# Sharing out the side work of a selective-scan kernel: by what is left of a unit instead of by a running credit

## The chip, the cores and the metric

The kernel runs on one core of one Trainium2 chip. The metric is device time in microseconds for one execution. The kernel before took 2837.61 us, the median of 3 runs that lie between 2833.27 and 2842.39 us.

## What is computed

The input has 2 sequences of 1024 tokens with 512 channels. A selective state-space layer with a state of 128 per channel comes first, then a residual and a layer normalisation, then a gated feed-forward layer of hidden width 2048, again with residual and normalisation. All of it is float32.

```
xn    = x * rsqrt(mean(x*x) + 1e-6) * norm_w
xn    = xn * sigmoid((xn @ select_proj_w.T + b) * select_gate)
xp    = xn @ x_proj_w.T                  # delta, B, C
delta = softplus(xp_delta @ dt_proj_w.T + dt_proj_b)
h     = exp(delta * A) * h + (delta * xn) * B      # for every token, 512 x 128 states
y     = sum over the state of h * C
x     = layernorm(x + (y + x * D_param) @ out_proj_w.T)
x     = layernorm(x + (silu(x @ w_gate.T) * (x @ w_up.T)) @ w_down.T)
```

## The kernel before, in words

**The scan and its places.** The 2048 tokens are cut into 64 steps of 32 tokens. A step has 16 pieces of work, so the main loop (L666 on, `for k in range(NG)`) runs 1024 times. One turn is called a place here, and its number modulo 8 is `r`; eight places are half a step. In each place TensorE (PE) makes the products `bu` (L689) and, for the next place, the decay exponents `a` (L407); ScalarE (ACT) takes their exponentials into `a_sb` (L414); VectorE (DVE) adds the carried state to the first column (L708) and runs one scan over 1024 elements (L709). GpSimd (POOL) spreads the operands (`ddt`, `du`, L378 and L388), one operation for each place. The two buffers of `bu` let PE work on the next place while DVE scans this one, and no further.

**The y products.** After a half's scans its outputs are summed by PE in `y_round` (L426): 12 matmuls at r = 1, 12 at r = 4 and 8 at r = 7 (`ROUNDS`). These three values of `r` get no side work.

**Side work.** Everything else on PE is written as generators: `pre` prepares the next lot of tokens (units ss, sel, xp, b, z, uT, t), `post` makes the layer's output for a tile of 128 tokens (units zT, op), `ffn` makes the feed-forward layer of that tile (units x1T, gu, d). A unit is one group of matmuls into the single PSUM tile `m` (pool `ps_m`, one buffer). It is cut into parts by `yield`: a `gu` unit has 8 parts of two matmuls, a `d` unit 16 parts of one, `op` 8, `sel`, `xp` and `ss` 4, `z` 2, the transposes 2, `t` 1. At the letter P a unit waits to be begun, at H it can go on, at E it waits for work of other engines, and what follows an E (the copy out of PSUM, the normalisation) is issued by `others` or `give_back` in a later place. A tile's post and ffn have 10 and 98 parts; a lot's `pre` has 39.

**How much in each place.** `work.tensor()` runs one part. It goes on with the unit that holds PE, or begins the first one that stands at P, and does nothing if the holder waits at an E; so at most one unit is in hand in a place. `PARTS` gives r = 0 four parts and r = 2, 3, 5 and 6 three each, 16 in eight places. What is not used stays as credit, up to 6, and at most 4 parts run in a place.

**Tiles and lots.** 64 places make one tile of 128 tokens. A lot has 256 tokens, two tiles, except the first two lots, which have one tile each. `pre` of the next lot is begun at a lot's first place, at the front of the list.

**The end.** After the last place the remaining y products are made, the rest of the list runs without places (L746, `while work.gens`), and the last tile's post and ffn end the program.

Of the kernel before, what the change touches and what calls it, by code (L numbers as in the profile page):

```python
# [18 lines left out]


ROUNDS = ((), (0, 1, 2), (), (), (3, 4, 5), (), (), (6, 7))
PARTS = (4, 0, 3, 3, 0, 3, 3, 0)
RMS_EPS = 1e-6
LN_EPS = 1e-5

# [9 lines left out]
def kernel(  # L35
# [25 lines left out]
    NF = wgu_s.shape[0]  # L61
    NM = D // P
# [79 lines left out]
    def col(group, m):  # L142
        return vec[:, group, m : m + 1]
# [10 lines left out]

    made = {}

    def misc(name):
        return bank_pool[0].tile([P, 512], FP, tag="m", name=name)


# [3 lines left out]
    def pre(c):  # L164

        t0, n = lots[c]
        n_j, n_s = n // P, n // S
# [15 lines left out]
        def matmuls(ps, w, m, rhs):  # L183
            for k in range(NM):
                nc.tensor.matmul(  # L185
                    ps[:, 0:n], w[:, k, ts(m, P)], rhs[:, k, :],
                    start=(k == 0), stop=(k == NM - 1),
                )
                yield "H" if k + 1 < NM else "E"
# [7 lines left out]
        for m in range(NM):  # L197
            nc.scalar.activation(xT[:, m, :], xT[:, m, :], AF.Copy, scale=col(V_NORM, m))
        yield "P"
        ps = misc(f"ss_{c}")  # L200
        for k in range(NM):
            nc.tensor.matmul(  # L202
                ps[:, 0:n], ones, u[:, k, :], start=(k == 0), stop=(k == NM - 1)
# [12 lines left out]


        for m in range(NM):
            ps = misc(f"sel_{c}_{m}")
            yield from matmuls(ps, sel_w, m, xn)  # L220
            nc.scalar.activation(
                u[:, m, :], ps[:, 0:n], AF.Relu,
                bias=neg[:, 1, m : m + 1], scale=neg[:, 0, m : m + 1],
            )
            nc.scalar.activation(
                dt[:, m, :], ps[:, 0:n], AF.Abs, bias=gate_b[:, m : m + 1], scale=col(V_GATE, m)
            )
            yield "P" if m + 1 < NM else "E"
# [9 lines left out]
            decay()  # L238

        for g, dst in ((0, low), (2, c_sb)):  # L240
            ps = misc(f"xp_{c}_{g}")
            yield from matmuls(ps, xp_w, g, xn)
            nc.scalar.copy(dst, ps[:, 0:n])
            yield "P"

        ps = misc(f"b_{c}")
        for j in range(n_j):
            for k in range(NM):
                nc.tensor.matmul(  # L249
# [12 lines left out]
        yield "P"  # L262

        for a in range(0, NM, 2):
            ps = misc(f"z_{c}_{a}")
            for m in (a, a + 1):
                nc.tensor.matmul(  # L267
                    ps[:, ts(m - a, n)], dt_w[:, ts(m, P)], low, start=True, stop=True
                )
                yield "H" if m == a else "E"  # L270
            for m in (a, a + 1):
                z = ps[:, ts(m - a, n)]
                nc.scalar.activation(u[:, m, :], z, AF.Relu, bias=col(V_DTB, m))
                nc.scalar.activation(dt[:, m, :], z, AF.Abs, bias=col(V_DTB, m))  # L274
            yield "P" if a == 0 else "E"
# [4 lines left out]

        for j in range(n_j):
            yield "P"
            ps = misc(f"uT_{c}_{j}")
            for m in range(NM):
                nc.tensor.transpose(ps[:, ts(m, P)], u[:, m, ts(j, P)], ident)
                if m == 1:
                    yield "H"
            yield "E"
            t = pre_pool.tile([P, D], FP, tag="row", name=f"uT_{c}_{j}")
            nc.scalar.copy(  # L290
                t.rearrange("p (g m c) -> p m g c", g=4, m=NM),
                ps.rearrange("p (m g c) -> p m g c", m=NM, g=4),
            )
            for st in range(4):
                nc.sync.dma_start(
                    ub_d[t0 // S + 4 * j + st, :, :, 0, :].rearrange("g t q -> t g q"),
                    t[ts(st, S), :].rearrange("t (g q) -> t g q", g=4),
                )
            if c == 0:
                load(0)  # L300
                diag(0, 0)
                diag(0, 1)
        yield "P"
        ps = misc(f"t0_{c}")
        for m in range(NM):
            nc.tensor.matmul(
                ps[0:n_s, ts(m, P)],
# [89 lines left out]
    def place(k):  # L397
        h, r = divmod(k, 8)
        m, pair = divmod(r, 2)
        return h, m, pair  # L400
# [47 lines left out]
    def post(tt):  # L448

        zT = post_pool.tile([P, NM, P], FP, tag="zT", name=f"zT_{tt}")  # L450
        nc.sync.dma_start(zT, x_q.rearrange("(m p) t -> p m t", p=P)[:, :, ts(tt, P)])
        yield "E"
        yield "E"
        nc.gpsimd.tensor_tensor(zT, zT, dq.unsqueeze(2).to_broadcast([P, NM, P]), ALU.mult)
        yield "E"
        yield "P"
        ps = misc(f"zT_{tt}")
        for s in range(4):
            nc.tensor.transpose(ps[:, ts(s, P)], yrs[tt][:, s, :], ident)
            if s == 1:  # L460
                yield "H"
        yield "E"
        z = zT.rearrange("p m (s t) -> p s m t", t=S)
        nc.vector.tensor_tensor(
            z, z, ps.rearrange("p (s m t) -> p s m t", m=NM, t=S), ALU.add
        )
        x1 = post_pool.tile([P, D], FP, tag="x1", name=f"x1_{tt}", bufs=4)
        nc.sync.dma_start(x1, xf[tt])
        yield "P"
        ps = misc(f"op_{tt}")  # L470
        for half in (slice(0, 256), slice(256, 512)):
            for k in range(NM):
                nc.tensor.matmul(  # L473
                    ps[:, half], zT[:, k, :], out_w[:, k, half], start=(k == 0), stop=(k == NM - 1)
                )
                yield "H" if half.start == 0 or k + 1 < NM else "E"
        nc.vector.tensor_tensor(x1, x1, ps, ALU.add)
        yield "E"
        yield from normalize(x1, f"a{tt}")
        work.add(ffn(tt, x1))  # L480

    def normalize(t, name):
# [10 lines left out]
    def ffn(tt, row):  # L493
# [17 lines left out]
        fetch(4)  # L511
        x1T = ffn_pool.tile([P, NM, P], FP, tag="x1T", name=f"x1T_{tt}")
        yield "P"
        ps = misc(f"x1T_{tt}")
        for m in range(NM):
            nc.tensor.transpose(ps[:, ts(m, P)], row[:, ts(m, P)], ident)
            if m == 1:
# [6 lines left out]
        for f in range(0, NF, 2):  # L524
            fetch(at + 4)
            yield "P"
            ps = misc(f"gu_{tt}_{f}")
            for b in range(2):
                w = pieces[at + b].rearrange("p (a k h) -> p a k h", a=2, k=NM)
                for a in range(2):  # L530
                    for k in range(NM):
                        nc.tensor.matmul(  # L532
                            ps[:, ts(2 * a + b, P)], w[:, a, k, :], x1T[:, k, :],
                            start=(k == 0), stop=(k == NM - 1),
                        )
                        if k % 2:
                            yield "E" if a and b and k + 1 == NM else "H"
            at += 2
            gu = ffn_pool.tile([P, 2, 2 * P], FP, tag="gu", name=f"gu_{tt}_{f}", bufs=2)
            nc.scalar.copy(gu, ps.rearrange("p (a t) -> p a t", a=2))  # L540
            work.add(silu(gu, hid[:, f : f + 2, :], f"{tt}_{f}", ready), front=True)
        while len(ready) < NF // 2:
            yield "E"
        for half in range(2):
            fetch(at + 4)
            yield "P"
            ps = misc(f"d_{tt}_{half}")
            for f in range(NF):
                if f == NH:
                    fetch(at + 6)  # L550
                w = pieces[at + f // 4].rearrange("p (f d) -> p f d", f=4)
                nc.tensor.matmul(  # L552
                    ps[:, 0:HD], hid[:, f, :], w[:, f % 4, :],
                    start=(f == 0), stop=(f == NF - 1),
                )
                yield "H" if f + 1 < NF else "E"
            part_of = row[:, ts(half, HD)]
            nc.vector.tensor_tensor(part_of, part_of, ps[:, 0:HD], ALU.add)
            at += 4
# [38 lines left out]
    class Work:  # L598


        def __init__(self):
            self.gens, self.holder = [], None

        def add(self, gen, front=False):
            item = [gen, next(gen)]
# [23 lines left out]
        def tensor(self):  # L629

            if self.holder is not None:
                if self.holder[1] != "H":
                    return False
                self.step(self.holder)
                return True
            for item in self.gens:
                if item[1] == "P":
                    self.holder = item
                    self.step(item)
                    return True  # L640
            return False

# [5 lines left out]
    work = Work()  # L648
# [13 lines left out]
    for b in range(2):  # L662
        decay_exp(0, b, decay_mm(0, b))

    pres, begun, credit = {}, set(), 0
    for k in range(NG):  # L666
        h, m, pair = place(k)
        st, i = divmod(h, 2)
        r = k % 8

        if PARTS[r]:
            work.give_back()
        if r == 0:
            hs[h] = half_pool.tile([P, 256, S], FP, tag="h", name=f"h_{h}")
            if i == 0:
                c = lot_of[st]
# [10 lines left out]
        for b in range(2):  # L687
            g = 2 * pair + b
# [26 lines left out]
        if h:  # L715
            for b in ROUNDS[r]:
                y_round(h - 1, b)
        credit = min(credit + PARTS[r], 6)
        for _ in range(min(credit, 4) if PARTS[r] else 0):
            if not work.tensor():  # L720
                break
            credit -= 1

        j, r4 = divmod(k, 4)
        if r4 == 3:
# [93 lines left out]
```

## Time and profile before

| what | us |
|---|---|
| profiled execution, device time | 2842.96 |
| its span, first to last instruction | 2841.2 |
| start of the first scan, start of the last scan | 43.2, 2758.35 |
| PE matmul busy | 2727.4 |
| DVE busy | 2522.9 |
| POOL busy | 1783.3 |
| ACT busy | 1549.8 |
| wait of DVE's add (L708) for PE's a (L407), in total | 80.2 |
| wait of PE's bu (L689) for DVE's scan (L709), in total | 28.3 |

The granted TensorE clock is 0.987 of full speed over the span. Busy time says how long an engine had an instruction in it; matmuls are pipelined, so PE's busy time is not work at its peak. The chain is followed back from the last instruction; its shares are of the span. In a timeline each row is one group of equal instructions that follow each other: start, duration, engine, line, operation, output and inputs, count; a float32 matmul shows as two records, so x16 is eight matmuls.

### The profile page before, as it was taken

The page shows a single profiled execution, that of the slowest core. Times are in us where ns is not written, and L with a number is a line of the kernel's source. Part 1 is how long each engine was busy: PE and PEld are TensorE (multiplying, and loading weights), DVE is VectorE, ACT ScalarE, POOL GpSimd, SP SyncE. Part 2 cuts the span into 40 slices and gives each one's busy share as a digit, 9 for nine tenths or more (in the row PEclk, how much of TensorE's full clock was granted, in tenths as well). Part 3 has the DMA queues.
Part 4 walks back from the last instruction along what each step waited for, and adds up shares of the span by engine and source line. Part 5 has one row for each costly group of instructions (what it writes and reads, how often), then busy time and mean ns, then how long its engine had stood idle before and what let it go on. Part 6 is the DMA issues. An engine that isn't in the chain of part 4 may idle for free.

```text
span 2841.2 us, 57463 instructions
## 1 busy us (share of the span) xinstructions
PE 2727.4 (96%) x22728; PEld 1484.1 (52%) x22728; DVE 2522.9 (89%) x2144; ACT 1549.8 (55%) x3105; POOL 1783.3 (63%) x2016
## 2 busy tenths in 40 slices
PE   7879999999999999999999999999999999999998
PEld 4324554555555554555544555555555555555558
DVE  2999898999999999999999999999999999999980
ACT  4546555555565455654656556555555554555442
POOL 4556675666667675775667667667576666657552
PEclk7999999999999999999999999999999999999999
DMA  2012222224223232233312333132331323332336
GB/s 75 16 30 66 86 77 79 87 73 134 86 62 116 86 121 64 83 96 105 123 43 84 105 104 104 57 100 93 112 101 47 113 87 109 101 105 96 107 103 208
DMA packets 112380, 258.67 MB, mean 91 GB/s; under 512 B 11568, under 2 KB 49456, under 8 KB 112112
## 3 DMA queue, kind: packets, MB, share of 16 engines
q1 hardware_dynamic: 112112, 254.99, 27.6%
q8 instruction: 181, 2.97, 0.4%
q14 instruction: 87, 0.71, 0.1%
HBM read 242.23 MB, written 12.71 MB: 90 GB/s over the span
## 4 chain that ended last, share of the span: by engine, by line
PE 75%; DVE 18%; issue 3%; ACT 2%; POOL 1%; DMA 0%; SPq 0%; DVEq 0%; POOLq 0%; ACTq 0%
PE bu L689 28%; PE gu L532 17%; DVE h L709 15%; PE y L426 13%; PE d L552 7%; PE a L407 4%; PE sel L185 2%; PE op L473 1%; PE xp L185 1%; DVE bu L708 1%; ACT a_sb L414 1%; PE b L249 1%; PE ss L202 0%; PE z L267 0%; DMA ub_d<-uT 0%
## 5 line engine op out<-in xcount | busy, mean ns | idle before, releaser
L709 DVE TENSOR_TENSOR_SCAN h<-a_sb,bu 128x1024 f32<-128x1024 f32 x1024 | 2341.2, 2287 | 159.2 <-POOL ddt L378 43.2
L414 ACT ACTIVATE a_sb<-a 128x496 f32<-128x496 f32 x2048 | 1089.0, 585 | 1142.6 <-PE a L407 1013.3
L689 PE MATMUL bu<-du,ub 32*128 32x512 f32 x4096 | 1198.0, 646 | 52.5 <-DVE h L709 28.3
L407 PE MATMUL a<-ddt,a_t 32*128 32x512 f32 x4096 | 1240.7, 646 | 2.8 <-ACT t L313 2.8
L378 POOL TENSOR_TENSOR ddt<-dt,hot 128x512 f32<-128x512 f32 x512 | 534.5, 1050 | 225.2 <-PE a L407 225.1
L532 PEld LDWEIGHTS gu<-x1T,w 128*128 128x128 f32 x4096 | 481.7, 192 | 232.8 <-issue 155.0
L388 POOL TENSOR_TENSOR du<-ub,hot 128x512 f32<-128x512 f32 x512 | 536.4, 1052 | 25.7 <-PE a L407 22.3
L532 PE MATMUL gu<-x1T,w 128*128 128x128 f32 x4096 | 537.3, 283 | 11.2 <-ACT t L313 4.5
L689 PEld LDWEIGHTS bu<-du,ub 32*128 32x128 f32 x4096 | 337.2, 184 | 375.8 <-issue 205.6
L426 PE MATMUL y<-h,cz 128*32 128x256 f32 x8192 | 524.7, 385 | 1.9 <-DVE h L709 1.3
L426 PEld LDWEIGHTS y<-h,cz 128*32 128x32 f32 x8192 | 227.7, 109 | 406.7 <-issue 271.9
L407 PEld LDWEIGHTS a<-ddt,a_t 32*128 32x128 f32 x4096 | 371.5, 184 | 19.9 <-ACT a_sb L414 9.6
L708 DVE TENSOR_TENSOR bu<-bu,cd 128x32 f32<-128x32 f32 x992 | 184.9, 186 | 83.1 <-PE a L407 80.2
L552 PE MATMUL d<-w,hid 128*128 128x256 f32 x1024 | 256.9, 393 | 1.1 <-ACT dt L274 1.1
L552 PEld LDWEIGHTS d<-w,hid 128*128 128x128 f32 x1024 | 183.5, 189 | 121.6 <-issue 92.5
L570 POOL TENSOR_SCALAR gu<-gu 128x256 f32<-128x256 f32 x128 | 108.3, 846 | 209.4 <-ACT gu L540 208.4
L578 POOL TENSOR_TENSOR hid<-gu,e 128x256 f32<-128x256 f32 x128 | 93.1, 728 | 141.7 <-ACT e L576 140.8
L440 POOL TENSOR_TENSOR yc<-yc,pick 128x512 f32<-128x512 f32 x64 | 66.7, 1042 | 168.7 <-ACT yc L439 168.7
L365 POOL TENSOR_TENSOR cd<-cd,h 128x256 f32<-128x256 f32 x124 | 106.5, 859 | 44.5 <-DVE h L709 44.5
L571 POOL TENSOR_TENSOR gu<-gu 128x256 f32<-128x256 f32 x128 | 93.4, 730 | 10.7
L540 ACT COPY gu<-gu 128x512 f32<-128x512 f32 x128 | 75.3, 588 | 33.5 <-PE gu L532 33.3
L323 POOL TENSOR_TENSOR dt<-dt,u 128x512 f32<-128x512 f32 (+1 forms) x36 | 41.3, 1151 | 68.7 <-ACT dt L320 68.7
(86 smaller groups left out, 1252.6 us busy)
## 6 DMA issues: line engine op xcount, KB each, us to landing
w<-in_wgu_s_dram SPq DMA_DIRECT2D x256, 512.0 KB, 3.8
w<-in_wd_s_dram SPq DMA_DIRECT2D x128, 512.0 KB, 4.0
cd<-dt_d SPq DMA_DIRECT2D x62, 256.0 KB, 4.0
ub<-ub_d SPq DMA_DIRECT2D x64, 128.0 KB, 2.0
ub_d<-bt SPq DMA_DIRECT2D x64, 64.0 KB, 1.8
ub_d<-uT SPq DMA_DIRECT2D x64, 64.0 KB, 1.8
zT<-in_x_q_dram SPq DMA_DIRECT2D x16, 256.0 KB, 4.0
x<-in_x_dram SPq DMA_DIRECT2D x16, 256.0 KB, 3.6
```

Of the source, the lines that this page charges most:

```text
L365: nc.gpsimd.tensor_tensor(cd, cd, last, ALU.mult)
L378: nc.gpsimd.tensor_tensor(ddts[j][:, m, :, :], made[lot_of[st]][0][:, a + m, toks(st)].unsqueeze(1).to_broadcast([P, 16, S]), hot[:, ts(i, ...
L388: nc.gpsimd.tensor_tensor(dus[j][:, m, :, :], uv[:, a + m, :].unsqueeze(2).to_broadcast([P, 16, S]), hot.unsqueeze(1).to_broadcast([P, 16, ...
L407: nc.tensor.matmul(ps, a_t[ts(g, 32), m, :], ddts[k // 4][ts(g, 32), m % 2, :, :], start=True, stop=True,)
L414: nc.scalar.activation(a_sb[:, k % 3, ts(b, 16), 1:], ps[:, :, 1:], AF.Exp, scale=-1.0)
L426: nc.tensor.matmul(ys[st][ts(m, 32), ts(i, 256)], cz[st % 3][:, at : at + 32], hs[h][:, ts(m, 64), ts(b, 4)], start=(i == 0 and b == 0), s ...
L532: nc.tensor.matmul(ps[:, ts(2 * a + b, P)], w[:, a, k, :], x1T[:, k, :], start=(k == 0), stop=(k == NM - 1),)
L552: nc.tensor.matmul(ps[:, 0:HD], hid[:, f, :], w[:, f % 4, :], start=(f == 0), stop=(f == NF - 1),)
L570: nc.gpsimd.tensor_scalar_max(g, g, -80.0)
L689: nc.tensor.matmul(bu[:, ts(b, 16), :], prepared[st][ts(g, 32), 1, :], dus[k // 4][ts(g, 32), m % 2, :, :], start=True, stop=True,)
L708: nc.vector.tensor_tensor(first, first, left[:, at : at + 2, i, :], ALU.add)
L709: nc.vector.tensor_tensor_scan(hs[h][:, ts(r, 32), :].rearrange("p q t -> p (q t)"), a_sb[:, k % 3, :, :].rearrange("p q t -> p (q t)"), b ...
```

## The change

Each unit now says how many parts it has when it takes its PSUM tile. A unit with four parts or less left, the one in hand among them, runs to its end in one go. A longer one runs four parts at r = 2 and 3, three at r = 5, 6 and 0, but four at r = 0 and 6 if it is begun there. The credit is gone. The matmuls, copies and transfers themselves are the same; their order on the engines is another.

```diff
-PARTS = (4, 0, 3, 3, 0, 3, 3, 0)
+PARTS = (3, 0, 4, 4, 0, 3, 3, 0)
...
-    def misc(name):
+    def misc(name, parts):
+        work.left = parts
         return bank_pool[0].tile([P, 512], FP, tag="m", name=name)
...
-            ps = misc(f"gu_{tt}_{f}")
+            ps = misc(f"gu_{tt}_{f}", 2 * NM)
...
-            ps = misc(f"d_{tt}_{half}")
+            ps = misc(f"d_{tt}_{half}", NF)
...
-            self.gens, self.holder = [], None
+            self.gens, self.holder, self.left, self.fresh = [], None, 0, False
...
             if self.holder is not None:
                 if self.holder[1] != "H":
                     return False
+                self.left -= 1
+                self.fresh = False
                 self.step(self.holder)
                 return True
             for item in self.gens:
                 if item[1] == "P":
                     self.holder = item
                     self.step(item)
+                    self.left -= 1
+                    self.fresh = True
                     return True
...
-        credit = min(credit + PARTS[r], 6)
-        for _ in range(min(credit, 4) if PARTS[r] else 0):
-            if not work.tensor():
-                break
-            credit -= 1
+        if PARTS[r] and work.tensor():
+            more = work.left
+            if more > 3:
+                more = (4 if work.fresh and r in (0, 6) else PARTS[r]) - 1
+            for _ in range(more):
+                work.tensor()
```

The other calls of `misc` get their counts in the same way (NM for ss, sel and xp, 2 for z and the transposes, 1 for t, 2 * NM for op).

More of the change, by code (lines that the diff above doesn't have):

```diff
@@ L199, in pre @@
         yield "P"
-        ps = misc(f"ss_{c}")
+        ps = misc(f"ss_{c}", NM)
         for k in range(NM):
@@ L218, in pre @@
         for m in range(NM):
-            ps = misc(f"sel_{c}_{m}")
+            ps = misc(f"sel_{c}_{m}", NM)
             yield from matmuls(ps, sel_w, m, xn)
@@ L240, in pre @@
         for g, dst in ((0, low), (2, c_sb)):
-            ps = misc(f"xp_{c}_{g}")
+            ps = misc(f"xp_{c}_{g}", NM)
             yield from matmuls(ps, xp_w, g, xn)
@@ L244, in pre @@
             yield "P"
-        ps = misc(f"b_{c}")
+        ps = misc(f"b_{c}", n_j)
         for j in range(n_j):
@@ L264, in pre @@
         for a in range(0, NM, 2):
-            ps = misc(f"z_{c}_{a}")
+            ps = misc(f"z_{c}_{a}", 2)
             for m in (a, a + 1):
@@ L282, in pre @@
             yield "P"
-            ps = misc(f"uT_{c}_{j}")
+            ps = misc(f"uT_{c}_{j}", 2)
             for m in range(NM):
@@ L303, in pre @@
         yield "P"
-        ps = misc(f"t0_{c}")
+        ps = misc(f"t0_{c}", 1)
         for m in range(NM):
@@ L456, in post @@
         yield "P"
-        ps = misc(f"zT_{tt}")
+        ps = misc(f"zT_{tt}", 2)
         for s in range(4):
@@ L469, in post @@
         yield "P"
-        ps = misc(f"op_{tt}")
+        ps = misc(f"op_{tt}", 2 * NM)
         for half in (slice(0, 256), slice(256, 512)):
@@ L513, in ffn @@
         yield "P"
-        ps = misc(f"x1T_{tt}")
+        ps = misc(f"x1T_{tt}", 2)
         for m in range(NM):
@@ L663 @@
         decay_exp(0, b, decay_mm(0, b))
-    pres, begun, credit = {}, set(), 0
+    pres, begun = {}, set()
     for k in range(NG):
```

## The prediction

> **What bounds the kernel now.** I read the page first: busy time and the chain.
>
> ```profile
> PE 2727.4 (96%) x22728; PEld 1484.1 (52%) x22728; DVE 2522.9 (89%) x2144; ACT 1549.8 (55%) x3105; POOL 1783.3 (63%) x2016
> ...
> PE 75%; DVE 18%; issue 3%; ACT 2%; POOL 1%; DMA 0%; SPq 0%; DVEq 0%; POOLq 0%; ACTq 0%
> ...
> L709 DVE TENSOR_TENSOR_SCAN h<-a_sb,bu 128x1024 f32<-128x1024 f32 x1024 | 2341.2, 2287 | 159.2 <-POOL ddt L378 43.2
> ...
> L708 DVE TENSOR_TENSOR bu<-bu,cd 128x32 f32<-128x32 f32 x992 | 184.9, 186 | 83.1 <-PE a L407 80.2
> ```
>
> The chain lies on PE and DVE in turn, so I look at single places: DVE's timeline around place 443, then PE's.
>
> ```profile
> 1226.66 2.29 DVE L709 TENSOR_TENSOR_SCAN h<-a_sb,bu 128x1024 f32<-128x1024 f32 x1
> ...
> 1229.71 2.29 DVE L709 TENSOR_TENSOR_SCAN h<-a_sb,bu 128x1024 f32<-128x1024 f32 x1
> ...
> 1232.21 2.29 DVE L709 TENSOR_TENSOR_SCAN h<-a_sb,bu 128x1024 f32<-128x1024 f32 x1
> ...
> 1234.82 2.29 DVE L709 TENSOR_TENSOR_SCAN h<-a_sb,bu 128x1024 f32<-128x1024 f32 x1
> ...
> 1237.30 2.29 DVE L709 TENSOR_TENSOR_SCAN h<-a_sb,bu 128x1024 f32<-128x1024 f32 x1
> ```
> ```profile
> 1226.18 2.05 PE L532 MATMUL gu<-x1T,w 128*128 128x128 f32 x16
> 1228.16 0.69 PE L689 MATMUL bu<-du,ub 32*128 32x512 f32 x1
> ...
> 1229.23 1.50 PE L426 MATMUL y<-h,cz 128*32 128x256 f32 x24
> 1230.67 0.69 PE L689 MATMUL bu<-du,ub 32*128 32x512 f32 x1
> ...
> 1231.74 1.60 PE L532 MATMUL gu<-x1T,w 128*128 128x128 f32 x12
> 1233.28 0.69 PE L689 MATMUL bu<-du,ub 32*128 32x512 f32 x1
> ...
> 1234.35 0.71 PE L532 MATMUL gu<-x1T,w 128*128 128x128 f32 x4
> ```
>
> A scan starts 1.55 after its place's first bu matmul (1228.16 to 1229.71). From scan to scan it is 3.05, 2.50, 2.61, 2.48: the first three follow PE's place (four parts, y, three parts), the last is DVE's own beat, for PE had only 1.71 of work. So I take:
> - DVE's beat: 2.483. Each tile adds its other DVE operations (L464, L477, L558, L587, L588), about 3.8, so 64 places need 64 x 2.483 + 3.8 = 162.7.
> - PE's place: 1.07 for bu and a, plus the side work: gu 1.71, 2.16, 2.605, 3.05 for one to four parts; d, op, sel, xp, ss 1.70, 2.13, 2.56, 3.00; y 2.50 (12) and 2.07 (8); transposes 1.66. That is 0.45 for a gu part and 0.19 for each start.
> - PE starts a bu no sooner than 0.06 after the scan two places back ends, so its lead over DVE is at most 2 x 2.483 - 2.287 - 0.06 - 1.55 = 1.07. A light place beyond that lead is lost; a heavy one past it is paid in full.
>
> Neither engine is the bound alone: PE's places sum to 2524 and DVE's needs to about 2587, yet the first scan's start to the last's is 2715.1.
>
> **The change part by part.** I went through both orders place by place with these rules, a unit also waiting until the one PSUM tile is copied out. For before this gives 2687.7. It misses 18.4 in the first 192 places and 9.0 in the other 831; this checks the rules.
>
> *Starts.* Places with side work fall from 600 to 588: 12 x 0.19 = 2.3 less on PE. In feed-forward alone this helps: eight places gu 2, 4, 4, 3, 3 parts take 20.8 where 4, 4, 4, 3, 1 took 21.1, since the single part (1.71) made a lead past 1.07.
>
> *What a tile gets.* A tile's post and ffn have 108 parts, a lot's pre 39. The credit gave 128 in 64 places, so the 147 of a lot's first tile spilled into the second (108). The new rule can give 17 to 20 in eight places: the first tile does all, the second runs short. PE's places then sum to 164.9 and 159.7 in 64, by turns, where before they lie near 161. 164.9 is over DVE's 162.7. The sum for places 256 to 319: 64 x 2.483 = 158.9, and over that 3.6 in places 257 to 269 (d, ss), 5.1 to 284 (d, zT, op, sel), 4.5 to 299 (xp, b, z, gu), 2.1 to 320: 174.1. Five such stretches measured 170.4 on average before: 5 x 3.65 = +18.3. Second tiles come to 167.65 against 168.52 measured in six stretches: -5.2. Places 896 on: +3.0 and +0.4. The missed 9.0 I let stand, since the waits it came from (ss, t behind its DMA) recur: 2223.5 against 2198.0, +25.5. The first 192 places: +3.7, less 2.4 that before paid at place 148 beyond my rule, because op was begun in the place after zT: +1.3.
>
> *Units next to each other.* Units begun in the place after one that DVE must copy out rise from 8 to 37 (d before zT, ss and x1T; op before sel and d). Before shows one at place 851:
>
> ```profile
> 2302.12 2.29 DVE L709 TENSOR_TENSOR_SCAN h<-a_sb,bu 128x1024 f32<-128x1024 f32 x1
> 2304.33 0.66 DVE L477 TENSOR_TENSOR x<-x,op 128x512 f32<-128x512 f32 x1
> ...
> 2306.13 2.29 DVE L709 TENSOR_TENSOR_SCAN h<-a_sb,bu 128x1024 f32<-128x1024 f32 x1
> ```
> ```profile
> 2305.04 2.05 PE L532 MATMUL gu<-x1T,w 128*128 128x128 f32 x16 [1.31 <-DVE x L477]
> ```
>
> The copy (L477) stands behind a scan, and bu and the next scan are queued behind the gu that waits: 1.31. The Trainium skill (Perfetto Trace Analysis, Optimizing Tensor Performance, Matmuls) says that independent groups should rotate through PSUM banks so that a copy overlaps the next group; one bank cannot, and the rule speaks against ends and starts in neighbouring places. Rule against rule the scans differ by 29.2 with these waits (26.8 once the 2.4 is off) and by 19.4 without, so they are 10 of it. I keep the row.
>
> *The end.* The new order leaves 12 d matmuls of tile 14 for after the last scan, before left 32 and a gu part.
>
> ```profile
> 2769.03 5.41 PE L473 MATMUL op<-out_w,zT 128*128 128x256 f32 x16 [1.39 <-DVE zT L464]
> 2774.27 13.98 PE L552 MATMUL d<-w,hid 128*128 128x256 f32 x64
> 2788.09 0.60 PE L516 MATMUL x1T<-ident,x 128*128 128x128 f32 x4
> ...
> 2790.74 1.65 PE L532 MATMUL gu<-x1T,w 128*128 128x128 f32 x6 [2.06 <-ACT x1T L520]
> ```
>
> d costs 13.98/32 = 0.437. On the same clock the y products still end at 2764.3; 12 d to 2769.5; its DVE work and zT's add to 2771.7; op, eight at 0.437, to 2775.2; the chain to the normalised row took 3.45 (op's end to x1T's source) and then x1T and its copy 1.4: gu starts at 2780.2, 10.5 sooner. But d no longer covers that chain, and the Trainium skill (TensorE: Matmul & The Clock Gate, Part 1) says an idle window of about 3.4 us halves PE's clock. Here 2769.0 to 2774.5 had a granted clock of 0.69 after the waits for zT, and 2791 to 2798 had 0.77: 1.7 each. The change fills the first wait and opens one of 3.5; by the rule alone I would add 1.7, by the row one slow window goes as one comes. I take -10.5, bounds -12 and -8.
>
> *Moved at no cost.* The w transfers go with their units: five buffers ahead and 3.8 us to land cover them; uncovered, a place would pay about 1.3. POOL's three silu operations (2.3 for a gu unit) come in pairs of places, before du and ddt; POOL is 63% busy. Weight loads wait 20.2 for du and 11.4 for ddt, matmuls hardly; if a fifth of that came to show it would be +6, and I take 0. ACT's copies (0.59) are as many as before.
>
> Sum: +25.5 + 1.3 - 10.5 = +16.3: 2842.96 becomes 2859, and the median 2837.61 becomes 2854.
>
> **The rivals.**
> - *PE is the bound throughout* (96% busy, 75% of the chain speak for it; scans at 2.48 with PE short speak against). Then only PE's own sum counts: 20 d and a gu part enter the places (+9.1), 12 starts leave (-2.3), the end gains 10.5: 2834, not slower.
> - *The lead carries the full tiles.* In the first tiles DVE already loses time at zT's and op's adds; if PE's excess falls there, they stay at 170.4 and the second tiles gain: -5.2 - 10.5 = 2822. It decides if first tiles come below 171.5. Against it: the lead is 1.07 and the excess comes in runs (d at 2 and 3: 3.00 twice).
> - *More waits.* Copies of z and t by ACT, POOL's pairs and neighbouring units may each cost a further 1 or so; 2.5 more a lot over seven lots: 2872. The nearest rows: bu's waits for a scan, 28.3 in all.
> - *It doesn't do what it says* is excluded: the orders differ as told.
>
> **How the numbers follow.** 2854 within 12 has 0.55; PE bound, 2834, 0.17; more waits, 2872, 0.18; the lead, 2822, 0.10. A measurement can tell about 0.3%, that is 2829 to 2846. Slower: 0.44 + 0.18; same: 0.11 of the first and 0.15 of the second; faster: 0.10 + 0.02. The range leaves out the lead's case and the top of the waits': 2830 to 2877.
>
> **What would show it.** In the profile after: 64-place stretches that take near 174 and 168 by turns; scan to scan 3.9 where op's add and the statistics stand together, and a side unit at r = 3 that waits over 1 for op's add; gu of the last tile starting about 22 after the last scan's start instead of 32. All stretches near 168 would make it wrong to the fast side, a first tile over 177 to the slow.

## The result and the profile after

The changed kernel takes 2855.61 us, the median of 4 runs (2854.23 to 2857.26), where before took 2836.88 (2833.27 to 2842.39). The ratio is 1.0065, with a 95% interval of 1.0047 to 1.0082: slower by 0.65%. The profiled execution took 2857.26, its span 2855.5. Lines of the changed kernel stand one to six higher (L715 is the scan, L714 the add, L533 gu, L553 d, L474 op, L478 and L559 DVE's adds behind op and d).

The page after, the lines that answer to those shown of before:

```profile
PE 2715.9 (95%) x22728; PEld 1471.0 (52%) x22728; DVE 2526.6 (88%) x2144; ACT 1544.0 (54%) x3105; POOL 1781.9 (62%) x2016
...
PE 71%; DVE 22%; issue 3%; ACT 2%; DMA 1%; POOL 0%; SPq 0%; DVEq 0%; ACTq 0%; POOLq 0%
...
L715 DVE TENSOR_TENSOR_SCAN h<-a_sb,bu 128x1024 f32<-128x1024 f32 x1024 | 2340.3, 2286 | 158.7 <-PE bu L695 43.8
...
L714 DVE TENSOR_TENSOR bu<-bu,cd 128x32 f32<-128x32 f32 x992 | 185.1, 187 | 102.2 <-PE a L408 99.8
```

The counts of instructions are those of before, and their durations nearly so. The span grew while PE was less busy; DVE's wait in front of its add rose from 83.1 to 102.2, and the chain runs over DVE more, over PE less. No engine got more instructions; they wait for each other more.

Where the time went, from the scans' starts (places 0, 64 and 1023) and the end of the span:

| stretch, us | before | after |
|---|---|---|
| first scan starts | 43.2 | 42.4 |
| places 0 to 63 | 165.6 | 159.3 |
| place 64 to the last scan's start | 2549.6 | 2580.2 |
| last scan's start to the end | 82.8 | 73.5 |

The first 64 places are the clock's doing and not the change's: in before's profile the granted clock was 0.5 from 39.6 to 70.4, in after's from 30.8 to 54.7, and places 4 to 7 take 2.75 each in the one and 2.2 in the other. The changed order run once more (with two row buffers, below) had the clock at 0.5 from 39.4 to 70.1, and its first 64 places took 167.4. I therefore compare profiles from place 64 on. There the change costs 30.6, and 9.3 of that comes back at the end.

Two places of the changed kernel show the new order, and what it costs there. In DVE's timeline around place 595, op ends at r = 2, so its add and the statistics stand in one lump before the next scan, and the d unit that begins at r = 3 waits for the add:

```profile
1630.06 2.29 DVE L715 TENSOR_TENSOR_SCAN h<-a_sb,bu 128x1024 f32<-128x1024 f32 x1
1632.26 0.66 DVE L478 TENSOR_TENSOR x<-x,op 128x512 f32<-128x512 f32 x1
1632.96 0.69 DVE L588 BATCH_NORM_STATS2 stats_a<-x 128x6 f32<-128x512 f32 x1
...
1634.06 2.29 DVE L715 TENSOR_TENSOR_SCAN h<-a_sb,bu 128x1024 f32<-128x1024 f32 x1
...
1636.55 2.29 DVE L715 TENSOR_TENSOR_SCAN h<-a_sb,bu 128x1024 f32<-128x1024 f32 x1
```
```profile
1628.84 1.99 PE L474 MATMUL op<-out_w,zT 128*128 128x256 f32 x8
...
1632.98 1.99 PE L553 MATMUL d<-w,hid 128*128 128x256 f32 x8 [1.08 <-DVE x L478]
```

From scan to scan it is 4.00 where 3.9 was forecast, all of it DVE's own work: the beat of 2.483 and 1.5 for the add and the statistics. The next scan follows after 2.49, so PE's wait of 1.08 was covered by the lead that this lump gave PE. In PE's timeline a few places earlier a d unit runs four and four at r = 2 and 3, then one part at r = 5, and zT follows in the next place and waits for d's copy:

```profile
1607.75 1.99 PE L553 MATMUL d<-w,hid 128*128 128x256 f32 x8
...
1610.75 1.99 PE L553 MATMUL d<-w,hid 128*128 128x256 f32 x8
...
1613.74 1.50 PE L427 MATMUL y<-h,cz 128*32 128x256 f32 x24
...
1616.25 0.70 PE L553 MATMUL d<-w,hid 128*128 128x256 f32 x2
...
1619.38 0.66 PE L460 MATMUL zT<-ident,yr 128*128 128x128 f32 x4 [0.77 <-DVE x L559]
```

DVE's timeline for the same places:

```profile
1608.31 2.29 DVE L715 TENSOR_TENSOR_SCAN h<-a_sb,bu 128x1024 f32<-128x1024 f32 x1
1610.92 0.20 DVE L714 TENSOR_TENSOR bu<-bu,cd 128x32 f32<-128x32 f32 x1 [0.33 <-PE a L408]
1611.22 2.29 DVE L715 TENSOR_TENSOR_SCAN h<-a_sb,bu 128x1024 f32<-128x1024 f32 x1
1613.92 0.20 DVE L714 TENSOR_TENSOR bu<-bu,cd 128x32 f32<-128x32 f32 x1 [0.41 <-PE a L408]
1614.22 2.29 DVE L715 TENSOR_TENSOR_SCAN h<-a_sb,bu 128x1024 f32<-128x1024 f32 x1
```

The two heavy places are paid: DVE waits 0.33 and 0.41 for PE. The wait of zT for d's copy is not: the light place at 1616.25 had put PE ahead, and the scans after it follow at DVE's own pace. So a wait in the list is not yet a loss.

The end of the changed kernel, PE's timeline and then the windows around it:

```profile
2787.85 5.45 PE L553 MATMUL d<-w,hid 128*128 128x256 f32 x24
...
2795.34 3.72 PE L474 MATMUL op<-out_w,zT 128*128 128x256 f32 x16 [1.61 <-DVE zT L465]
...
2802.56 1.12 PE L517 MATMUL x1T<-ident,x 128*128 128x128 f32 x4 [3.50 <-ACT x L490]
...
2804.35 10.86 PE L533 MATMUL gu<-x1T,w 128*128 128x128 f32 x74 [0.68 <-ACT x1T L521]
```
```profile
2795.00:2800.00 5.00, 3.72 (x16) 2.96 (x16) 1.15 (x3) 1.05 (x3) 0.26 (x1) 1.00 0.53 154
2800.00:2804.00 4.00, 1.12 (x4) 0.72 (x4) 0.70 (x2) 1.60 (x4) 0.27 (x1) 0.80 1.01 409
2804.00:2811.00 7.00, 6.65 (x38) 6.65 (x39) 0.00 (x0) 0.74 (x2) 0.00 (x0) 0.62 0.40 147
```

In a window row the last three columns are granted clock, DMA share and GB/s. op now runs on the full clock (3.72 instead of 5.41), and the wait of 3.50 for the normalised row is followed by a slow window: x1T takes 1.12 instead of 0.60. gu starts 22.4 after the last scan's start, before 32.4.

### The profile page after: what moved, and what is told of

It reads as the page before. It is cut to its first block, busy times and chain, and to the rows that moved or that the text cites. A ratio compares the mean times of both kernels' runs of the same rounds, so it can differ in the third digit from the quotient of the medians.

```text
span 2855.5 us, 57418 instructions
## 1 busy us (share of the span) xinstructions
PE 2715.9 (95%) x22728; PEld 1471.0 (52%) x22728; DVE 2526.6 (88%) x2144; ACT 1544.0 (54%) x3105; POOL 1781.9 (62%) x2016
## 4 chain that ended last, share of the span: by engine, by line
PE 71%; DVE 22%; issue 3%; ACT 2%; DMA 1%; POOL 0%; SPq 0%; DVEq 0%; ACTq 0%; POOLq 0%
PE bu L695 26%; DVE h L715 19%; PE gu L533 17%; PE y L427 12%; PE d L553 7%; PE a L408 4%; PE sel L186 2%; DVE bu L714 1%; PE xp L186 1%; ACT a_sb L415 1%; DMA ub_d<-uT 1%; PE b L250 1%; PE op L474 1%; PE z L268 1%; PE ss L203 0%
## 5 line engine op out<-in xcount | busy, mean ns | idle before, releaser
L715 DVE TENSOR_TENSOR_SCAN h<-a_sb,bu 128x1024 f32<-128x1024 f32 x1024 | 2340.3, 2286 | 158.7 <-PE bu L695 43.8
L533 PEld LDWEIGHTS gu<-x1T,w 128*128 128x128 f32 x4096 | 482.6, 193 | 229.6 <-issue 176.7
L533 PE MATMUL gu<-x1T,w 128*128 128x128 f32 x4096 | 537.0, 283 | 11.7 <-ACT t L314 8.8
L389 POOL TENSOR_TENSOR du<-ub,hot 128x512 f32<-128x512 f32 x512 | 535.6, 1049 | 15.9 <-PE a L408 12.4
L408 PEld LDWEIGHTS a<-ddt,a_t 32*128 32x128 f32 x4096 | 363.8, 184 | 18.6 <-ACT a_sb L415 10.1
L714 DVE TENSOR_TENSOR bu<-bu,cd 128x32 f32<-128x32 f32 x992 | 185.1, 187 | 102.2 <-PE a L408 99.8
L553 PE MATMUL d<-w,hid 128*128 128x256 f32 x1024 | 258.9, 393 | 8.8 <-DVE x L478 6.5
L553 PEld LDWEIGHTS d<-w,hid 128*128 128x128 f32 x1024 | 182.8, 189 | 135.1 <-issue 95.2
L572 POOL TENSOR_TENSOR gu<-gu 128x256 f32<-128x256 f32 x128 | 93.0, 727 | 10.7
L353 POOL TENSOR_TENSOR cd<-a_n,cd 128x512 f32<-128x512 f32 x62 | 78.9, 1272 | 0.0
```

What stands on the lines that cost most here:

```text
L389: nc.gpsimd.tensor_tensor(dus[j][:, m, :, :], uv[:, a + m, :].unsqueeze(2).to_broadcast([P, 16, S]), hot.unsqueeze(1).to_broadcast([P, 16, ...
L408: nc.tensor.matmul(ps, a_t[ts(g, 32), m, :], ddts[k // 4][ts(g, 32), m % 2, :, :], start=True, stop=True,)
L533: nc.tensor.matmul(ps[:, ts(2 * a + b, P)], w[:, a, k, :], x1T[:, k, :], start=(k == 0), stop=(k == NM - 1),)
L553: nc.tensor.matmul(ps[:, 0:HD], hid[:, f, :], w[:, f % 4, :], start=(f == 0), stop=(f == NF - 1),)
L714: nc.vector.tensor_tensor(first, first, left[:, at : at + 2, i, :], ALU.add)
L715: nc.vector.tensor_tensor_scan(hs[h][:, ts(r, 32), :].rearrange("p q t -> p (q t)"), a_sb[:, k % 3, :, :].rearrange("p q t -> p (q t)"), b ...
```

## The experiments

All times from place 64 to the last scan's start are of one profile of the run. "Sum" is the prediction's place-by-place sum on that kernel's own order, with the 20 added that it missed on before (24 in the last two kernels without a second buffer). "Neighbours" are units begun in the place after one that DVE copies out. The theories named "sharing", "pair" and so on are those of the expectations.

**Old places, units in one go.** The new kernel with the old places and the old credit; the credit may be overdrawn to end a unit.

```diff
-PARTS = (3, 0, 4, 4, 0, 3, 3, 0)
+PARTS = (4, 0, 3, 3, 0, 3, 3, 0)
...
-        if PARTS[r] and work.tensor():
+        credit = min(credit + PARTS[r], 6)
+        if PARTS[r] and credit > 0 and work.tensor():
             more = work.left
             if more > 3:
-                more = (4 if work.fresh and r in (0, 6) else PARTS[r]) - 1
+                more = min(credit, 4) - 1
             for _ in range(more):
                 work.tensor()
+            credit -= 1 + more
```

> The old places and the old credit (4, 3, 3, 3, 3; 16 parts in eight places), but a unit with four parts or less left runs in one go and what it takes too much is owed. Measured: from place 64's scan to the last one before takes 2549.6 and after 2580.2. Theory 'sharing' (the change loses because it does a lot's preparation all in the first tile and leaves the second short, the rest being units next to each other): here the supply stays at 128 parts for 64 places and neighbours behind a DVE copy are 12 (before 8, after 40), so the place-by-place sum gives 2541, and the stretches stay between 166 and 170 instead of 168 and 175 by turns; the end is 9 to 11 shorter as in after; total about 2818, faster than both. Theory 'goes' (running units in one go is itself the loss, since it makes heavier places): slower than before, about as after, 2850 or more.

Measured: 2826.97 us, ratio to before 0.9966 (0.9952 to 0.9979). From place 64 it takes 2549.7, as long as before, where 2541 was expected; the end takes 71.4, 11.4 less. "Goes", which asked for 2850 or more, falls. But the equal times hide two differences: places 64 to 191 take 343.0 here and 351.6 before (6.4 of that at places 110 to 113, where before waits once for t), and from place 192 on it is 2206.7 against 2198.0. So in the regular tiles this kernel is 8.7 longer than before.

**New places, old credit.** Before, with only the new `PARTS`.

```diff
-PARTS = (4, 0, 3, 3, 0, 3, 3, 0)
+PARTS = (3, 0, 4, 4, 0, 3, 3, 0)
```

> The old credit with the new places only (3, 4, 4, 3, 3; 17 in eight places, 4 at r = 2 and 3). Theory 'sharing': 17 in eight places is 136 for 64 places against 127.5 needed, so the list runs dry a little less unevenly than in after; but neighbours behind a DVE copy are 30 and 4 parts stand in two places in a row; the sum from place 64 gives 2583 (after: 2580), total about 2860. If the loss were only in the uneven stretches, these would come out near 170 all along and the total near 2840. Theory 'goes': faster than after, near before.

Measured: 2857.9 us, ratio 1.0073 (1.0061 to 1.0086), from place 64 2580.3 (expected 2583). One line of the change makes the whole loss over the scans. That line moves the fours and also raises the parts in eight places from 16 to 17.

**The new rule with 16 parts in eight places.** The changed kernel with an account that earns as before did.

```diff
-        if PARTS[r] and work.tensor():
+        credit = min(credit + (4, 0, 3, 3, 0, 3, 3, 0)[r], 6)
+        if PARTS[r] and credit > 0 and work.tensor():
...
+            credit -= 1 + more
```

> The new rule with a budget: 16 parts are earned in eight places as before, a go is made only if the account is above nothing, and it may be overdrawn. It takes the uneven supply out and keeps the goes and the places 4 at r = 2 and 3. Theory 'sharing': stretches of 169.5 and 171 by turns instead of 174 and 168, neighbours 15 instead of 40; from place 64 to the last scan 2567 (after 2580, before 2550); total about 2845, a good third of the loss over the scans back. Theory 'goes' or 'places' (4 parts in two places running): no more than 2 or 3 of it back, total 2853 or more.

Measured: 2856.82 us, ratio 1.0076 (1.0063 to 1.0089), from place 64 2580.3. The stretches are evener, 171.6 to 175.2 and, after one of 167.1, 171.3 to 173.3 by turns, and nothing is gained: five first tiles save 7.7 against the change, six second ones lose 18.6, and the places from 896 on save 8.9. Evening the supply brings nothing back in total, which speaks against "sharing"; but the account also leaves places without side work and puts op behind zT, so it is not a test of the supply alone. Here the sum was 13 too low (11 waits of op for zT's add, 12.6 in all, are part of it).

**No unit beside one that DVE copies out.** Begins at P are refused in the place after the last part of zT, op or d.

```diff
+            if self.main and self.dve and self.k == self.last + 1:
+                return False
             for item in self.gens:
```

> The new rule, but no unit is begun in the place after one that DVE copies out of PSUM (zT, op, d). This costs parts: one whole gate-and-up part of a tile (16 groups of eight matmuls, 30.5) and its d are left for the end, so the end is some 31 longer than before and the total about 2850. What counts is the stretch from place 64 to the last scan, per matmul done there: 46.6 of PE's places less than in after. Theory 'neighbours behind DVE's copy cost what was predicted' (10 of the loss): waits of side units for L478, L559 and L465 all but vanish and the sum gives 2531, that is 49 less than after. If the neighbours cost nothing, the stretch falls only by what DVE did not hide of the work left out, to 2545 or more.

Measured: 2849.62 us, ratio 1.0049 (1.0037 to 1.0061). From place 64 it is 2531.1, exactly the sum, and the units' waits for DVE's adds are gone from the list of waits. But 46.6 of PE's work is gone from the stretch too and the end is 113.1, so this run alone does not price the neighbours; the run with ACT's copies, below, does.

**Three parts at r = 3.** The changed kernel with one number changed.

```diff
-PARTS = (3, 0, 4, 4, 0, 3, 3, 0)
+PARTS = (3, 0, 4, 3, 0, 3, 3, 0)
```

> The new rule with one number changed: three parts instead of four at r = 3, so PARTS is (3, 0, 4, 3, 0, 3, 3, 0). First runs: old places with goes 2549.7 from place 64 to the last scan, new places with the old credit 2580.3, new rule with a budget 2580.3, new rule 2580.2, before 2549.6; so what is common to the slow ones is the places, not the supply. New theory 'pair' (four parts at r = 2 and again at r = 3, with the 12 y matmuls before and after, use up PE's lead of 1.07 and every further bit is paid; it also sets units to end where DVE's copy is in the way): about 30 back, 2541 to 2550, total about 2819, though PE's places sum to 3 more than in after and the end is the same. Theory 'sharing' of the prediction (a lot's first tile takes all the preparation): PE's places are still 163.1 and 161.9 by turns here and the supply is one part less, so half of it at best, 2565, total 2842.

Measured: 2825.46 us, ratio 0.9957 (0.9945 to 0.997), faster than both kernels. From place 64 2550.0: all 30 back. First and second tiles still differ, 172.9 and 167.6 on average, but by the expectation PE's places sum to 163.1 and 161.9, nearly even where the change had 164.9 and 159.7; so this number took away most of the uneven supply, one of the two fours and 26 of the 40 neighbours at once. From place 192 on it is 2207.1, 21.7 less than the change and 9.1 more than before; the rest came at places 64 to 191. Its list of waits has only one row over 1 us in which a unit waits for DVE, op for zT's add, which stands beside it now:

```profile
PE bu L695 <- DVE bu L714: 21.3, 42, 1.6
PE bu L695 <- DVE h L715: 20.7, 32, 1.3
PE op L474 <- DVE zT L465: 17.0, 14, 2.1
```

**Four at r = 3 alone, and four at r = 2 and 5.**

```diff
-PARTS = (3, 0, 4, 4, 0, 3, 3, 0)
+PARTS = (3, 0, 3, 4, 0, 3, 3, 0)
```
```diff
-PARTS = (3, 0, 4, 4, 0, 3, 3, 0)
+PARTS = (3, 0, 4, 3, 0, 4, 3, 0)
```

> The new rule with three parts at r = 2 and four at r = 3: (3, 0, 3, 4, 0, 3, 3, 0). Supply as in the run with four at r = 2 only. If the pair is what costs, both runs with one four gain alike, 2545 to 2550 from place 64. If a four at r = 3 costs by itself (behind it stand y's 12 at r = 4, no light place comes before r = 7), or if the units that end and begin next to each other count (21 here, 14 with the four at r = 2, 40 in after), this one stays slow: the place-by-place sum gives 2562. The end has 22 gate-and-up matmuls more than before instead of 20 d less, about 3 longer than before; total 2852 by the sum, 2836 by 'pair alone'.

> The new rule with the two fours apart: (3, 0, 4, 3, 0, 4, 3, 0), so the same 17 parts in eight places as in after, with y's 12 and a three between them. Neighbours behind DVE's copy are 8, as few as before. 'Pair' with the lead: the fours are apart, so the waste between them is less, and the sum gives 2566 from place 64 (after 2580), total about 2845; what is left is because a y place (2.50) and a three (2.6) give no lead back, only r = 7 does. If neighbours were the whole loss: 2550.

Measured: 2858.48 us for the one, ratio 1.0076 (1.0061 to 1.0092), from place 64 2568.2, and an end of 84.8; 2844.3 for the other, ratio 1.003 (1.002 to 1.0041), from place 64 2565.1. Both came out within 7 of the sum. One four at r = 3 costs 18 more than one four at r = 2, though only 6 of it from place 192 on, so "pair alone" did not hold as forecast; and eight neighbours with 2565 show that neighbours are not all.

**ACT copies out.** The changed order is kept; ACT copies the results of zT, op and d into SBUF, DVE adds from there.

```diff
-        nc.vector.tensor_tensor(x1, x1, ps, ALU.add)
+        held = post_pool.tile([P, D], FP, tag="held", name=f"ho_{tt}")
+        nc.scalar.copy(held, ps)
+        nc.vector.tensor_tensor(x1, x1, held, ALU.add)
```

> The new rule with its order kept, but ACT copies zT's, op's and d's result out of PSUM into SBUF and DVE adds from there, so the next unit no longer waits for DVE behind its scan. This adds 64 ACT copies of 0.4 to 0.6 and leaves DVE's work as it is. Prediction's step: the waits of units for DVE are 10 of the loss, so from place 64 to the last scan 2570 (after 2580), total about 2846. If these waits are hidden anyway: 2580 and 2856. If ACT's copies stand before the exponentials and delay the scans: above 2580.

Measured: 2848.33 us, ratio 1.0042 (1.003 to 1.0054), from place 64 2570.3: 9.9 less than the change, where 10 was the prediction's price for the neighbours. The changed kernel's list of waits, the rows where a unit waits for DVE (total, times, longest), and then the head of the list with ACT copying:

```profile
PE sel L186 <- DVE x L478: 7.5, 6, 1.3
PE d L553 <- DVE x L478: 6.5, 6, 1.1
PE zT L460 <- DVE x L559: 5.4, 7, 0.8
...
PE ss L203 <- DVE x L559: 4.4, 6, 0.8
...
PE x1T L517 <- DVE x L559: 4.1, 6, 0.9
PE d L553 <- DVE x L559: 2.3, 3, 0.8
```
```profile
PE bu L701 <- DVE h L721: 34.5, 64, 2.2
PE bu L701 <- DVE bu L720: 25.6, 49, 2.2
PE gu L537 <- ACT t L314: 9.3, 7, 2.9
PE bu L701 <- POOL du L389: 7.5, 7, 1.2
```

The six rows sum to 30.2 and are gone. But 9.9 is a net gain, for DVE's work did not stay as it was. Its page, beside the 2526.6 that DVE was busy in the change:

```profile
PE 2714.2 (95%) x22728; PEld 1469.6 (52%) x22728; DVE 2537.7 (89%) x2144; ACT 1571.0 (55%) x3169; POOL 1786.3 (63%) x2016
```

d's add takes 0.40 in the change, also where POOL is at work on ddt. With both its inputs in SBUF it takes 1.16 in 15 of 32 cases, all of them begun 0.17 after such a POOL operation, and 0.40 to 0.46 in the others:

```profile
1618.76 1.05 POOL L379 TENSOR_TENSOR ddt<-dt,hot 128x512 f32<-128x512 f32 x1 [3.45 <-PE a L408]
1618.93 0.40 DVE L559 TENSOR_TENSOR x<-x,d 128x256 f32<-128x256 f32 x1
```
```profile
1614.63 1.05 POOL L379 TENSOR_TENSOR ddt<-dt,hot 128x512 f32<-128x512 f32 x1 [3.44 <-PE a L408]
1614.80 1.16 DVE L565 TENSOR_TENSOR x<-x,hd 128x256 f32<-128x256 f32 x1
```

The adds of the three units sum to 47.0 where they were 33.9, and bu waits 7.5 for du (0.3 in the change). So by this run the neighbours cost 9.9 or more; as an estimate, 23 if all of the 13.1 that the adds grew lay on the path.

**Three at r = 3 for d alone, and for all but d.**

```diff
-                more = (4 if work.fresh and r in (0, 6) else PARTS[r]) - 1
+                most = 3 if work.wide and r == 3 else PARTS[r]
+                more = (4 if work.fresh and r in (0, 6) else most) - 1
```

`work.wide` is set where a unit has 16 parts, as d has. The kernel for all but d has `not work.wide` in its place.

> The new rule, only that a d unit runs three parts instead of four at r = 3; gu, op and all else keep four at r = 2 and 3. Theory 'd' (d cut 3, 4, 4, 1, 4 leaves a single part at r = 5 and the next unit beside DVE's copy): most of the 30 back, 2550 from place 64 to the last scan (sum of places 2526 and the 24 it has missed), total about 2825. Theory 'pair' (two fours in a row are dear wherever they stand): only the d half of it back, 13 to 20, 2560 to 2567, since gu's pairs stay, total 2838. Neighbours behind DVE's copy are 15.

> The reverse: d keeps four at r = 2 and 3, and every other unit longer than four parts (gu, op) runs three at r = 3. Theory 'd': nothing or little back, 2575 or more. Theory 'pair': the gu half of it, 2565. Theory 'lock' (neither four is dear by itself; the new rule with these places falls into a round of 64 places in which d, op and zT always end and begin side by side, 40 such neighbours, and any change of one place breaks that round): the place-by-place sum gives 2528 and so about 2552, nearly all back, with 20 neighbours, total about 2827.

Measured: 2835.44 us for d alone, ratio 1.0002 (0.999 to 1.0013), from place 64 2556.4; 2828.24 for the others, ratio 0.9975 (0.9963 to 0.9987), from place 64 2547.0. Changing one half of the pairs brings 24 back, changing the other half 33, and both together 30. These do not add, so the pairs have no fixed price each. "Lock" forecast this, with 15 and 20 neighbours instead of 40; but the kernel with 16 parts in eight places has 15 neighbours too and got nothing back, so a broken round is not enough. All kernels with one row buffer and DVE's copies, with the places that run four parts counted from place 64 on:

| kernel | from 64 | of it from 192 | neighbours | places with four parts |
|---|---|---|---|---|
| before | 2549.6 | 2198.0 | 8 | 300 |
| the change | 2580.2 | 2228.8 | 40 | 310 |
| old places, one go | 2549.7 | 2206.7 | 12 | 288 |
| new places, old credit | 2580.3 | 2233.0 | 30 | 346 |
| new rule, 16 in eight | 2580.3 | 2230.9 | 15 | 321 |
| three at r = 3 | 2550.0 | 2207.1 | 14 | 247 |
| four at r = 3 alone | 2568.2 | 2213.1 | 21 | 283 |
| four at r = 2 and 5 | 2565.1 | 2223.0 | 8 | 344 |
| d alone three | 2556.4 | 2209.9 | 15 | 260 |
| all but d three | 2547.0 | 2204.5 | 20 | 262 |

(The run without neighbours is left out, since it does less work there.) From place 192 on the neighbours do not order the kernels, but the last column parts them: 2223 or more with 310 such places or more, 2213 or less with 300 or fewer. That fits the prediction's lead, by which a heavy place is paid and a light one beyond the lead lost; no run changes this count alone, so it is a candidate and not shown.

To see where the loss lies, I charged each scan-to-scan time, less the beat of 2.483 and less DVE's other operations before that scan, to the last side unit that PE ran before it:

| us from place 64, by unit | before | after | three at r = 3 | d alone | all but d | ACT copies |
|---|---|---|---|---|---|---|
| d | 22.0 | 33.4 | 13.0 | 13.3 | 19.5 | 35.2 |
| gu | 74.7 | 83.6 | 68.9 | 79.0 | 63.5 | 82.5 |
| op | 8.7 | 1.3 | 18.7 | 9.7 | 15.4 | 1.5 |
| sel, ss, xp | 8.7 | 20.6 | 13.0 | 16.8 | 12.9 | 9.8 |
| all | 117.4 | 147.9 | 117.5 | 123.8 | 114.5 | 137.7 |

The change loses 11 at d, 9 at gu and 12 at the preparation, and gains 7 at op, since zT and op no longer stand side by side. With ACT copying the preparation gains, where sel and ss followed op and d; d's 35.2 counts the adds at their old length, and with their own length there it is some 12 less than that.

**Two row buffers**, in the fast version and in the change.

```diff
-            t = pre_pool.tile([P, D], FP, tag="row", name=f"uT_{c}_{j}")
+            t = pre_pool.tile([P, D], FP, tag="row", name=f"uT_{c}_{j}", bufs=2)
```

The line for t's copy gets the same `bufs=2`.

> The fast version, three at r = 3 in the new rule, with two buffers for the tile row, into which ACT copies uT and t: there t's copy waits for uT's DMA to leave the one buffer, with the exponentials queued behind it on ACT, and PE's next gu waits for t (8.6 in 7 waits). The order is the same. If that wait is on the path: some 6 to 8 off the 2550, total about 2818. If it is hidden: 2825 as before it.

> The change as it is, with two buffers for the tile row (uT's and t's copies). With three parts at r = 3 the second buffer took 16 off from place 64 to the last scan (2550.0 to 2534.0), where 6 to 8 were expected from the waits of PE alone. If that wait (t's copy behind uT's transfer, the exponentials behind it on ACT) is a cost of its own beside the shares, it goes here too: 2580.2 to about 2565, total about 2840, and the shares' loss of 30 stays as it is. If it was part of what the change lost, more than 20 comes back; if the new order hid it, less than 5.

Measured: 2816.71 us, ratio 0.9931 (0.9916 to 0.9945), and 2847.76, ratio 1.0034 (1.0023 to 1.0045). From place 64: 2534.0 and 2567.8, so 16.0 and 12.4 less. The two orders still lie 33.8 apart (30.2 with one buffer), so it is a cost beside the shares. The changed kernel's waits, first without and then with the second buffer:

```profile
PEld gu L533 <- ACT t L314: 14.1, 7, 3.1
ACT t L314 <- DMA ub_d<-uT: 13.7, 6, 3.3
...
PE gu L533 <- ACT t L314: 8.8, 7, 2.9
```
```profile
PEld gu L533 <- ACT t L314: 5.5, 7, 1.0
...
ACT t L314 <- PE t L307: 2.4, 2, 1.2
```

ACT's wait for the transfer is gone, and the matmuls' own wait for t falls from 8.8 to 0.7. 4.0 of either gain lies at place 111, where the second lot's t is awaited by the main loop. The clock may have a share: from place 64 to the last scan it was granted at 0.5 for 23.9 in both kernels with one buffer, and for 6.8 and 17.1 with two.

## Why the prediction was right, and where its reason was not

**The total.** 2854 was forecast and 2855.6 measured. Per stretch it was less exact: from place 64 the scans lose 30.6, while the sum had 26.8 for the whole scan; the end gives 9.3 of the 10.5 forecast. 6.3 that the profiles show at the start belongs to the clock of two single executions; without it they would give 21.3 where the medians give 18.7, and 2.6 stays unexplained. That the total came out within 2 is partly luck, since the largest term of the sum did not hold as a cause.

**PE and DVE share the bound, with a lead of 1.07.** This held. The sum on each kernel's own order ranked the kernels roughly: where a sum stands on record from place 64 it was, without the 20 added, 17 to 33 below what was measured (20 for before). A spread of 16 is half of the loss that it was to explain. What it leaves out is waits behind ACT and POOL, the row buffer's among them.

**What a tile gets.** This step is not borne out as the cause. It said that the credit's end gives the first tile of a lot everything and leaves the second short, and put +18.3 and -5.2 on that. The signs were right: five first tiles lost 22.8, six second tiles gained 2.6, half of the 5.2. But an account that evens the supply leaves 2580.3. What the runs show in its place is the new places: 30.7 with the old credit (2580.3 against 2549.6) and 30.6 with goes and an account of 16 (2580.3 against 2549.7). From place 192 on the two are 35.0 and 24.2, so the agreement is partly luck. The fast version cannot decide, since it is nearly even in PE's places; uneven supply may still have a part in what neighbours do not explain.

**Starts.** Twelve fewer starts were put at 2.3 less on PE. That cannot be seen beside the rest; running in one go came out at nothing over the scans in total (2549.7 against 2549.6) and at 8.7 more from place 192 on. Its use is at the end: 4 or 12 d matmuls are left for it where 32 were.

**Units next to each other.** Priced at 10, with 40 of them where 37 were counted. ACT's copies brought 9.9 back, net of adds that took 13.1 longer, so 10 is the least they cost and the agreement is partly luck. The rule that the Trainium skill gives (Perfetto Trace Analysis, Optimizing Tensor Performance, Matmuls), to rotate groups through PSUM banks, fits this: freeing the bank sooner gained. No run here rotates banks.

**Moved at no cost.** The weight loads' wait for du rose from 20.2 to 25.1 in the list, and the matmuls' own waits for du and ddt are not among its twenty largest rows, so 0 was fair. But ACT's wait for a transfer, which the prediction let stand, was worth 12.4.

**The last tiles.** Places 896 on were put at +3.4 and measured +10.7. The list runs dry there: places 966 to 970 and 978 to 980 have no side work. PE then waits for DVE, and the granted clock halves in the windows that follow: 1.9 is lost at place 970 and 1.5 at 981, where the 12 y matmuls take 2.79 instead of 1.50.

```profile
2623.90:2631.80 7.90, 5.30 (x41) 2.00 (x40) 7.62 (x8) 4.29 (x11) 1.31 (x2) 1.00 0.01 2
2631.80:2638.60 6.80, 6.20 (x40) 2.35 (x41) 5.30 (x5) 2.67 (x5) 4.95 (x7) 0.50 0.36 116
```
```profile
2630.01 0.66 PE L695 MATMUL bu<-du,ub 32*128 32x512 f32 x1 [1.49 <-DVE bu L714]
...
2632.40 1.22 PE L695 MATMUL bu<-du,ub 32*128 32x512 f32 x1 [1.25 <-DVE h L715]
...
2634.42 2.79 PE L427 MATMUL y<-h,cz 128*32 128x256 f32 x24
```

The sum knew of the empty places but not of the clock.

**The end.** gu started 22.4 after the last scan where 21.8 was forecast. Here the Trainium skill (TensorE: Matmul & The Clock Gate, Part 1), which asks for an idle window of about 3.4 us, agrees with the changed kernel: one slow window of 6.8 after 3.5 of waiting. It does not agree with the others: before's two slow windows of 3.4 came after waits of 2.01 and 1.39 with work between them, and after one of 2.06; and ahead of place 970 PE was busy for 5.30 of the 7.90 before the clock fell. The measurement decides: shorter waits were enough. I let one window stand for one, which is 6.8 against 6.8 in all.

**The rivals.** "PE is the bound throughout" gave 2834 and falls: PE's places sum to 3 more with three at r = 3 than in the change (2534 against 2531), and the scans take 30 less. "The lead carries the full tiles" asked for first tiles below 171.5; they take 173.8 to 176.1. "More waits", at 2872, is not what was measured.

**What stays open.** Why exactly the places 3, 4, 4, 3, 3 lose 30.6: neighbours are at least 9.9 of it, and the rest is not split between the number of heavy places, the supply, the clock and the round. The clock was at 0.5 for 13.7 from place 64 to the last scan before and for 23.9 after, about 5 of the loss at most (an estimate: half of the difference), the two places named among it. The charge shows where DVE waits, not what would cure it. Whether before gains from a second row buffer was not tried.

## What to carry to other kernels

Where two engines hand work to each other through two buffers, a schedule is worth what its heavy and light places do to the lead (1.07 here, less than half a place), and the sum of work per engine says little: a version with 3 more on PE was 30 faster. Test such a scheduler by its order on the engines, changing one number at a time, since two changes that each took the loss away did not add here. Compare the regular stretch as well as the total: a gain in the first tiles, most of it at one wait, hid a loss of 8.7 in one kernel. With one PSUM bank for side work, look at what ends just before each unit begins, and who copies it out; and where a copy moves an add's input, time the add again.

## What the runs showed that I had not expected

The second row buffer took off 12.4 and 16.0, while the matmuls' own waits for t are 8.8 in the list: ACT waits 13.7 for the transfer before t's copy, and the exponentials issued behind it have to wait too. How the gain divides between them and the clock was not tried.

The first 64 places took 159.1 to 167.4 in the profiles of kernels whose start is nearly the same; the granted clock was 0.5 for 17 to 31 us from 30 to 40 us on, at other times in each execution. In before's PE had a matmul in it for all of these 30.8 us, and the clock stayed at 0.5.
